# Third attention of a fused four-layer kernel: one reciprocal of few rows for both key blocks, and gathers issued a pair of batches sooner

## The chip, the cores and the metric

The kernel runs on one core of one Trainium2 chip. The metric is the device time of one launch in microseconds; lower is better. Three timed runs of the kernel before are at hand, and one further execution that the hardware profiler took.

## The reference, cut to what matters

The program applies four layers of cross attention and feed-forward to `x` of shape 16 x 128 x 256. The change lies in the attention of the third layer (`L2`), whose input is `x` after the mixture of experts of the second layer has been added to it:

```
q = LN(x @ Wq + bq)                 # 16 heads of 16 channels
k, v         from the first 112 context tokens
k_dca, v_dca from the last  16 context tokens
ctx     = softmax(q k^T / 4)     v          # one softmax over 112 keys
ctx_dca = softmax(q k_dca^T / 4) v_dca      # a second one over 16 keys
x = x + (ctx + ctx_dca) @ Wo + bo
```

So each head of each query has two softmax sums, one for each block of keys, and both outputs have to be divided by their own sum before the output projection adds them. The experts' result reaches `x` by a gather: each token has two rows in a scratch tensor in HBM, and both are added with their weights.

## The kernel before, in words

A stage follows a stage, and in each a Python loop goes over the 16 batches of 128 tokens. Five engines (PE, DVE, ACT, POOL, SP) each work through their own list in order. The framework that builds the kernel chooses each list's order from the program order, from free buffers and from an estimate of its own; so an instruction may stand earlier or later in its list than the code reads.

In the third attention (`l2_attn`) the batch is cut into two halves `c` of eight heads each; within a half, `j` is one of two groups of four heads. For each half:

- `l2_terms` makes the scores `S` of eight heads on PE (in the only buffer of its pool[...]), takes the maxima `mx` of both key blocks and subtracts them on DVE into `E`, and ACT takes the exponent.
- `l2_heads` turns `E` on PE (`pT`), ACT copies it out (`eT`), and PE multiplies it by the values into `po[:, 0]` and by a tile `own` of ones into `po[:, 1]`. The rows of `po` are channels: 32 for each head, 16 of the block of 112 keys and 16 of the block of 16 keys. `own` repeats each sum over its 16 channels, so that the reciprocal `rz` on DVE has a value for every channel (128 x 256), and the product `oT` is one multiplication.
- `l2_out` multiplies `oT` by `Wo` and adds it to `x`.

Around them, `front(b + 3)` makes `qk` and `vx` of a later batch. DVE adds the bias, ACT squares it (`sq`), DVE sums it (`r`) and takes an inverse root in some ten small steps, and POOL scales `qk`. `turn(b + 2)` turns `qk` on PE (`pqkT`), ACT copies it out (`qkT`) and POOL spreads the keys over four heads (`kbd`), from which the next `S` is made. After each even batch `l2_inputs` prepares two more batches. `combine` gathers the experts' rows `moe_y` on the POOL queue (two buffers) and adds them on DVE; then come the statistics `st` and `mv`, the inverse root `rs` on POOL, `xn` on DVE and the turn `pxT` on PE.

Of the kernel before, what the change touches and what calls it, by code (L numbers as in the profile page):

```python
# [8 lines left out]
F32 = mybir.dt.float32  # L9
# [6 lines left out]
ALU = mybir.AluOpType  # L16
# [4 lines left out]
P = 128  # L21
D = 256
# [23 lines left out]
def bc(ap, axis, n):  # L46
    u = ap.unsqueeze(axis)
    shape = list(u.shape)
    shape[axis] = n
    return u.to_broadcast(shape)  # L50


class Net:
# [778 lines left out]
    def l1_ffn(self, w, after, ctx):  # L832
        nc, tc = self.nc, self.tc
# [4 lines left out]
        with ExitStack() as es:  # L838
            op = es.enter_context(tc.tile_pool(name="f1o", bufs=1))
            bp = es.enter_context(tc.tile_pool(name="f1b", bufs=3))  # L840
            sp = es.enter_context(tc.tile_pool(name="f1s", bufs=2))
            tr = es.enter_context(tc.tile_pool(name="f1tr", bufs=3, space=PSUM))
# [145 lines left out]
                pass  # L988
            for _ in late:
                pass  # L990
            self.l2_inputs(0, tr)
            for bs in groups[3:]:
                for _ in shared(bs):
                    pass

    def combine(self, pool, b):

        nc = self.nc
        y = pool.tile([P, 2, D], F32, tag="moe_y", name=f"moe_y{b}")
        for k in range(2):  # L1000
            nc.gpsimd.indirect_dma_start(
                out=y[:, k, :], out_offset=None, in_=self.back,
                in_offset=bass.IndirectOffsetOnAxis(ap=self.slot[:, k, b : b + 1], axis=0),
            )
        for k in range(2):
            nc.vector.scalar_tensor_tensor(
                self.x[b], y[:, k, :], self.pk[:, k, b : b + 1], self.x[b], ALU.mult, ALU.add
            )


    def l2_setup(self, ctx, w):

        nc, tc = self.nc, self.tc
        Wq = w[:, 0:512].rearrange("p (c n) -> p c n", c=2)
        Wm = w[:, 512:1024]
        Wd = w[:, 1024:1536]
        op = ctx.enter_context(tc.tile_pool(name="l2o", bufs=1, side="right"))
        self.l2x = ctx.enter_context(tc.tile_pool(name="l2x", bufs=2, side="right"))

        cd = op.tile([P, B, P], F32, tag="cd", name="cd")  # L1020
        nc.gpsimd.memset(cd, 0.0)
        nc.gpsimd.tensor_copy(cd[:, :, 112:P], self.ctxT[:, :, 112:P])
        nc.gpsimd.memset(self.ctxT[:, :, 112:P], 0.0)

        bqk = op.tile([P, 32, 16], F32, tag="bqk", name="bqk")
        flat = bqk.rearrange("p h d -> p (h d)")

        bv = op.tile([P, 2, 256], F32, tag="bv", name="bv")
        nc.gpsimd.memset(bv, 0.0)
        for t, name, skip, part in (  # L1030
            (flat[:, 256:512], "bkv_main", 0, slice(0, 112)), (flat[:, 256:512], "bkv_dca", 0, slice(112, P)),
            (bv[:, 0], "bkv_main", 256, slice(0, 112)), (bv[:, 1], "bkv_dca", 256, slice(112, P)),
        ):
            at = ROWS[name][0] + skip
            nc.scalar.dma_start(
                out=t[part], in_=self.a["rows"][at : at + 256].partition_broadcast(part.stop - part.start)
            )
        norms = op.tile([P, 6], F32, tag="norms", name="norms")
        nc.scalar.dma_start(out=norms, in_=self.a["norms2"])

        own = op.tile([P, 2, 16], F32, tag="own", name="own")
        nc.gpsimd.tensor_copy(own, self.consts[:, 16:18].unsqueeze(2).to_broadcast([P, 2, 16]))
        nc.vector.tensor_copy(flat[:, 0:256], self.row("bq2"))

        for t in (Wq[:, 0], Wq[:, 1], Wm[:, 0:256], Wd[:, 0:256], flat[:, 0:256], flat[:, 256:512]):
            t3 = t.rearrange("p (h d) -> p h d", h=16)
            m = op.tile([P, 16], F32, tag="wm", name="wm", bufs=2)
            nc.vector.tensor_reduce(m, t3, AX.X, ALU.add)
            nc.vector.tensor_scalar_mul(m, m, 1.0 / 16)
            nc.vector.tensor_tensor(t3, t3, bc(m, 2, 16), ALU.subtract)  # L1050
        self.l2_const = cd, flat, bv, norms, own
        self.l2_xT = {}

    def l2_inputs(self, g, psum):

        bs = [b for b in range(2 * g, 2 * g + 2) if b < self.nb]
        if bs:
            for b in bs:
                self.combine(self.l2x, b)
            xT = self.lnT(self.l2x, psum, bs, rsqrt=self.rsqrt_pool)[1]  # L1060
            for i, b in enumerate(bs):
                self.l2_xT[b] = xT[:, :, i * P : (i + 1) * P]

    def l2_attn(self, w):
        nc, tc = self.nc, self.tc
# [4 lines left out]
        with ExitStack() as es:  # L1070
            sp = es.enter_context(tc.tile_pool(name="l2s", bufs=3))
# [2 lines left out]
            sc = es.enter_context(tc.tile_pool(name="l2sc", bufs=1, space=PSUM))  # L1074
            tr = es.enter_context(tc.tile_pool(name="l2tr", bufs=3, space=PSUM))
            pvp = es.enter_context(tc.tile_pool(name="l2pv", bufs=1, space=PSUM))
            cd, flat, bv, norms, own = self.l2_const
            vp = es.enter_context(tc.tile_pool(name="l2v", bufs=1))
            vx = [vp.tile([P, 16, 2, 16], F32, tag=f"vx{k}", name=f"vx{k}") for k in range(3)]
            xTs, normed, ready = self.l2_xT, {}, {}  # L1080

# [74 lines left out]
            b = self.nb - 1  # L1156
# [28 lines left out]
    def l2_heads(self, sp, ep, tr, pvp, b, c, Es, vx, own, oT):  # L1185

        nc = self.nc
        po = pvp.tile([P, 2, 2, P], F32, tag="po", name=f"po{b}_{c}")
        eTs = []
        for j in range(2):  # L1190
            pT = self.transposes(tr, lambda i: Es[:, j, i, :], 4, f"pT{b}_{c}_{j}")
            eT = ep.tile([P, 4, P], F32, tag="eT", name=f"eT{b}_{c}_{j}", bufs=3)
            nc.scalar.copy(eT, pT)
            eTs.append(eT)
        for j in range(2):
            for of in range(2):
                for i in range(4):
                    stand = own if of else vx[:, 8 * c + 4 * j + i]
                    nc.tensor.matmul(
                        po[32 * i : 32 * i + 32, of, j, :], stand.rearrange("p s d -> p (s d)"), eTs[j][:, i, :],  # L1200
                        start=True, stop=True,
                    )
        rz = sp.tile([P, 2, P], F32, tag="rz", name=f"rz{b}_{c}", bufs=2)
        nc.vector.reciprocal(rz, po[:, 1])  # L1204
        nc.vector.tensor_tensor(oT[:, 2 * c : 2 * c + 2], po[:, 0], rz, ALU.mult)

    def l2_out(self, mm, b, oT, Wo):
        nc = self.nc
# [489 lines left out]
def pack(np, i):  # L1698
# [5 lines left out]
    cat = lambda *x: np.ascontiguousarray(np.concatenate(x, axis=1))  # L1704
    o = {}
# [61 lines left out]
    for name, v in (  # L1767
# [3 lines left out]
    ):  # L1771
        row[ROWS[name][0] : ROWS[name][0] + len(v)] = v
    o["rows"] = row

    o["norms2"] = np.ascontiguousarray(np.stack([
        np.tile(i[f"L2_xattn_{k}"], 8) for k in ("qn_w", "qn_b", "kn_w", "kn_b", "kn_dca_w", "kn_dca_b")
# [9 lines left out]
    c = np.zeros((P, 18), np.float32)  # L1786
# [27 lines left out]
```

## Time and profile before

| | |
|---|---|
| runs, us | 2497.4, 2489.95, 2499.14 (median 2497.4) |
| profiled execution | 2492.25 us, span 2490.5 us, mean granted clock 0.974 |
| busy in the span: PE, DVE, ACT, POOL | 2281.8, 1723.0, 1048.2, 746.9 us |
| from the first to the last reciprocal of the stage | 1395.1 to 1613.7 us |
| reciprocal `rz` of the stage | 32 of 128x256, 1744 ns each |
| multiplication `oT` | 32 of 128x256, 409 ns each |
| gathers `moe_y` | 32, 968 ns each on POOL, 2.8 us to landing |

The page gives busy time of each engine in the span and the costliest groups of instructions by their line. The trace can be cut to a window of time, and asked in it for the busy time of each engine, for what each instruction waited for, and for the instructions in order. A busy PE is not PE at its peak, since matmuls overlap one another. In this trace one product of float32 stands as two rows of PE.

### The profile page before, as it was taken

Reading aid. Unit: us, or ns where it says so; the run is one execution under the profiler, and the core shown is the slowest. Engines: PE = TensorE matmul, PEld = TensorE weight load, DVE = VectorE, ACT = ScalarE, POOL = GpSimd, SP = SyncE. Lnnn points to the kernel's source line nnn. Section 1 sums busy time; section 2 is a strip of 40 time slices with the busy share of each in tenths; the row PEclk is TensorE's granted clock in tenths of the full one; section 3 lists DMA queues with packets and bytes.
Section 4 is the critical chain, followed back from the end, with each engine's and each line's share of the span. In section 5 each row is a group of like instructions: output and inputs, shape, how many; then the busy total and the mean of one; then the engine's idle time right before and its main releaser. Section 6 shows DMA issues by size and latency. Waiting matters only on the chain. (4 is left out here: it accounts for less than half of the span.)

```text
span 2490.5 us, 39604 instructions
## 1 busy us (share of the span) xinstructions
PE 2281.8 (92%) x14876; PEld 1709.7 (69%) x14876; DVE 1723.0 (69%) x3904; ACT 1048.2 (42%) x2778; POOL 746.9 (30%) x678
## 2 busy tenths in 40 slices
PE   6999799999989999998997778899899999999798
PEld 3666589898977777775884455555577777776465
DVE  6888788888865555565574999831466666668964
ACT  3656455455533443432331333411455555554121
POOL 3222234343411322222002433100222332224665
PEclk8999899999999999998999899999999999999999
DMA  9000200000030000002223000000100000000000
GB/s 376 17 2 2 86 1 1 1 1 1 1 121 2 19 10 10 10 13 84 69 71 137 25 14 10 1 0 1 69 1 1 1 1 1 1 1 1 7 13 15
DMA packets 29678, 74.57 MB, mean 30 GB/s; under 512 B 6688, under 2 KB 21160, under 8 KB 23856
## 3 DMA queue, kind: packets, MB, share of 16 engines
q1 hardware_dynamic: 25200, 62.06, 6.7%
q0 software_dynamic: 3072, 8.39, 1.0%
q8 instruction: 119, 1.95, 0.3%
q10 hardware_dynamic: 1216, 1.59, 0.2%
q14 instruction: 71, 0.58, 0.1%
HBM read 46.07 MB, written 25.95 MB: 29 GB/s over the span
## 5 line engine op out<-in xcount | busy, mean ns | idle before, releaser
L501 POOL TENSOR_TENSOR g<-sim 128x1024 f32<-128x1024 f32 x64 | 140.2, 2212 | 221.1 <-ACT sim L466 186.4
L181 PE MATMUL pT<-ident,E 128*128 128x128 f32 x1280 | 196.0, 283 | 9.8 <-POOL E L631 7.5
L511 DVE SCALAR_TENSOR_TENSOR g<-g,th 128x1024 f32<-128x1024 f32 x128 | 194.3, 1577 | 0.0
L181 PEld LDWEIGHTS pT<-ident,E 128*128 128x128 f32 x1280 | 147.0, 144 | 51.7 <-issue 21.8
L507 ACT ACTIVATE g<-sim 128x128 f32<-128x128 f32 x512 | 159.8, 390 | 32.0 <-PE r L525 31.5
L626 ACT ACTIVATE E<-E,mx 128x128 f32<-128x128 f32 x256 | 99.5, 390 | 160.1 <-DVE mx L623 138.7
L1464 POOL TENSOR_TENSOR E<-E,rs 128x512 f32<-128x512 f32 x64 | 66.6, 1041 | 302.0 <-DVE rs L1463 148.6
L1459 ACT ACTIVATE E<-S,mx,sc 128x128 f32<-128x128 f32 x256 | 113.9, 455 | 98.8 <-DVE mx L1455 89.6
L525 PE MATMUL r<-ident,g 128*128 128x128 f32 x1024 | 124.6, 277 | 19.9 <-DVE g L511 19.8
L525 PEld LDWEIGHTS r<-ident,g 128*128 128x128 f32 x1024 | 115.4, 142 | 27.7 <-DVE g L511 17.5
L661 PE MATMUL py<-w_w_l,oT 128*128 128x256 f32 x512 | 128.1, 383 | 5.2 <-DVE x L663 3.6
L1492 PE MATMUL py<-w_w_l,oT 128*128 128x256 f32 x512 | 131.1, 383 | 0.1
L1492 PEld LDWEIGHTS py<-w_w_l,oT 128*128 128x128 f32 x512 | 93.6, 190 | 46.9 <-issue 39.2
L631 POOL TENSOR_TENSOR E<-E,rs 128x512 f32<-128x512 f32 x64 | 66.7, 1042 | 193.5 <-DVE rs L630 119.8
L417 PE MATMUL fh<-xnT,w_w_f 128*128 128x128 f32 x1024 | 122.7, 279 | 0.0
L600 PE MATMUL pt<-xnT,w_w_l 128*128 128x256 f32 x512 | 121.1, 382 | 0.0
L661 PEld LDWEIGHTS py<-w_w_l,oT 128*128 128x128 f32 x512 | 93.9, 190 | 39.4 <-issue 20.1
L417 PEld LDWEIGHTS fh<-xnT,w_w_f 128*128 128x128 f32 x1024 | 118.6, 194 | 1.8
L538 PE MATMUL fy<-w_w_f,wT 128*128 128x256 f32 x512 | 118.4, 379 | 0.0
L1406 PE MATMUL pq<-xnT,w_w_l 128*128 128x256 f32 x512 | 116.2, 380 | 1.0 <-ACT xnT L67 0.6
L600 PEld LDWEIGHTS pt<-xnT,w_w_l 128*128 128x128 f32 x512 | 94.9, 192 | 15.2 <-issue 2.5
L1406 PEld LDWEIGHTS pq<-xnT,w_w_l 128*128 128x128 f32 x512 | 94.8, 190 | 14.4 <-ACT sqk L1372 1.2
(401 smaller groups left out, 5505.7 us busy)
## 6 DMA issues: line engine op xcount, KB each, us to landing
w_w_f<-in_w_f SPq DMA_DIRECT2D x14, 1024.0 KB, 11.2
sent<-zero SPq DMA_DIRECT2D x14, 1024.0 KB, 20.2
w_w_l<-in_w_l SPq DMA_DIRECT2D x14, 1024.0 KB, 11.1
xb<-sent SPq DMA_DIRECT2D x38, 128.0 KB, 2.0
back<-yb SPq DMA_DIRECT2D x38, 128.0 KB, 1.9
x<-in_x SPq DMA_DIRECT2D x16, 128.0 KB, 4.9
out<-x SPq DMA_DIRECT2D x16, 128.0 KB, 1.7
ctx<-in_ctx ACTq DMA_DIRECT2D x1, 1024.0 KB, 8.4
```

Of the source, the lines that this page charges most:

```text
L181: self.nc.tensor.transpose(ps[:, i, :], src(i), self.ident)
L417: nc.tensor.matmul(ps[:, k, :], down[:, c, a * P : (a + 1) * P], xT[:, c, :], start=c == 0, stop=c == 1)
L501: nc.gpsimd.tensor_tensor(g, bc(sim[:, 2 * h, 8 * half : 8 * half + 8], 2, P), bc(sim[:, 2 * h + 1, :], 1, 8), ALU.add)
L507: nc.scalar.activation(g[:, k, :], sim[:, 2 * h + 1, :], AF.Identity, bias=sim[:, 2 * h, a : a + 1])
L511: nc.vector.scalar_tensor_tensor(gf, gf, th[:, h : h + 1], gf, ALU.is_ge, ALU.mult)
L525: nc.tensor.matmul(ps[:, k, :], G[h][:, 4 * q + k, :], self.ident, start=h == 0, stop=h == 3, is_transpose=True)
L538: self.nc.tensor.matmul(py, wT[:, k, :], up[:, a, :], start=a == 0, stop=a == 15)
L600: nc.tensor.matmul(ps[:, k], A[:, h + k, c, :], xT[:, c, :], start=c == 0, stop=c == 1)
L661: nc.tensor.matmul(pys[b], oT[:, j, :], Wo[:, h, :], start=h == 0, stop=h == 15)
L1406: nc.tensor.matmul(ps[:, l], Wq[:, c, h * P : (h + 1) * P], xT[:, c, :], start=c == 0, stop=c == 1)
L1459: nc.scalar.activation(E[:, j, :], S[:, j, :], AF.Exp, bias=mx[:, j : j + 1], scale=sc[:, i, 0, r, j : j + 1], accum_out=rs[:, j : j + 1],)
L1492: nc.tensor.matmul(pys[b], oT[:, j, :], Wo[:, h, :], start=h == 0, stop=h == 15)
```

## The change

Two things change, both inside the third attention.

First, the sums. A tile `sums` that is loaded from HBM takes the place of `own`. Its first part makes PE write the sums of one head into 4 of its 32 rows only (two groups `j` times two key blocks), accumulating both `j` into one tile `po[:, 2]` of 128 x 128. DVE takes the reciprocal of this half-sized tile. Its second part, `spread`, is a matrix of ones and zeros: two more products on PE carry the inverses from those rows to the channels, into a PSUM tile `pr` of the pool that the turns use too. Meanwhile ACT copies the unscaled output from `po[:, 0:2]` to `oT`, and DVE multiplies `pr` by `oT`.

Second, the gathers. `combine` no longer issues its own. `fetch` issues the gathers of a pair of batches when the pair before has been combined, and the first pair's ahead of `l2_inputs(0)`.

```diff
+            self.fetched = {}
+            self.fetch(self.l2x, 0)
             self.l2_inputs(0, tr)
...
+    def fetch(self, pool, g):
+
+        for b in range(2 * g, min(2 * g + 2, self.nb)):
+            y = self.fetched[b] = pool.tile([P, 2, D], F32, tag="moe_y", name=f"moe_y{b}")
+            for k in range(2):
+                self.nc.gpsimd.indirect_dma_start(
+                    out=y[:, k, :], out_offset=None, in_=self.back,
+                    in_offset=bass.IndirectOffsetOnAxis(ap=self.slot[:, k, b : b + 1], axis=0),
+                )
+
+    def combine(self, b):
 
         nc = self.nc
-        y = pool.tile([P, 2, D], F32, tag="moe_y", name=f"moe_y{b}")
-        for k in range(2):
-            nc.gpsimd.indirect_dma_start(
-                out=y[:, k, :], out_offset=None, in_=self.back,
-                in_offset=bass.IndirectOffsetOnAxis(ap=self.slot[:, k, b : b + 1], axis=0),
-            )
+        y = self.fetched.pop(b)
...
-        own = op.tile([P, 2, 16], F32, tag="own", name="own")
-        nc.gpsimd.tensor_copy(own, self.consts[:, 16:18].unsqueeze(2).to_broadcast([P, 2, 16]))
...
             for b in bs:
-                self.combine(self.l2x, b)
+                self.combine(b)
+            self.fetch(self.l2x, g + 1)
             xT = self.lnT(self.l2x, psum, bs, rsqrt=self.rsqrt_pool)[1]
...
+            sums = vp.tile([P, 320], F32, tag="sums", name="sums")
+            nc.scalar.dma_start(out=sums, in_=self.a["sums2"])
+            own = (
+                sums[:, 0:64].rearrange("p (j n) -> p j n", j=2), sums[:, 64:320].rearrange("p (j n) -> p j n", j=2)
+            )
...
-        po = pvp.tile([P, 2, 2, P], F32, tag="po", name=f"po{b}_{c}")
+        own, spread = own
+        po = pvp.tile([P, 4, P], F32, tag="po", name=f"po{b}_{c}")
...
         for j in range(2):
-            for of in range(2):
-                for i in range(4):
-                    stand = own if of else vx[:, 8 * c + 4 * j + i]
-                    nc.tensor.matmul(
-                        po[32 * i : 32 * i + 32, of, j, :], stand.rearrange("p s d -> p (s d)"), eTs[j][:, i, :],
-                        start=True, stop=True,
-                    )
-        rz = sp.tile([P, 2, P], F32, tag="rz", name=f"rz{b}_{c}", bufs=2)
-        nc.vector.reciprocal(rz, po[:, 1])
-        nc.vector.tensor_tensor(oT[:, 2 * c : 2 * c + 2], po[:, 0], rz, ALU.mult)
+            for i in range(4):
+                nc.tensor.matmul(
+                    po[32 * i : 32 * i + 32, j, :], vx[:, 8 * c + 4 * j + i].rearrange("p s d -> p (s d)"),
+                    eTs[j][:, i, :], start=True, stop=True,
+                )
+        for j in range(2):
+            for i in range(4):
+                nc.tensor.matmul(
+                    po[32 * i : 32 * i + 32, 2, :], own[:, j], eTs[j][:, i, :], start=j == 0, stop=j == 1
+                )
+        rz = sp.tile([P, P], F32, tag="rz", name=f"rz{b}_{c}", bufs=2)
+        nc.vector.reciprocal(rz, po[:, 2])
+        nc.scalar.copy(oT[:, 2 * c : 2 * c + 2], po[:, 0:2])
+        pr = tr.tile([P, 2, P], F32, tag="tr", name=f"pr{b}_{c}")
+        for j in range(2):
+            nc.tensor.matmul(pr[:, j], spread[:, j], rz, start=True, stop=True)
+        nc.vector.tensor_tensor(oT[:, 2 * c : 2 * c + 2], pr, oT[:, 2 * c : 2 * c + 2], ALU.mult)
```

The two constant tables that `sums` holds are packed on the host, beside the other weights.

More of the change, by code (lines that the diff above doesn't have):

```diff
@@ L994, in l1_ffn @@
                     pass
-    def combine(self, pool, b):
-        nc = self.nc
-        y = pool.tile([P, 2, D], F32, tag="moe_y", name=f"moe_y{b}")
-        for k in range(2):
-            nc.gpsimd.indirect_dma_start(
-                out=y[:, k, :], out_offset=None, in_=self.back,
-                in_offset=bass.IndirectOffsetOnAxis(ap=self.slot[:, k, b : b + 1], axis=0),
-            )
+    def fetch(self, pool, g):
[7 more added lines that the diff above has]
+    def combine(self, b):
+        nc = self.nc
+        y = self.fetched.pop(b)
         for k in range(2):
@@ L1050, in l2_setup @@
             nc.vector.tensor_tensor(t3, t3, bc(m, 2, 16), ALU.subtract)
-        self.l2_const = cd, flat, bv, norms, own
+        self.l2_const = cd, flat, bv, norms
         self.l2_xT = {}
@@ L1076, in l2_attn @@
             pvp = es.enter_context(tc.tile_pool(name="l2pv", bufs=1, space=PSUM))
-            cd, flat, bv, norms, own = self.l2_const
+            cd, flat, bv, norms = self.l2_const
             vp = es.enter_context(tc.tile_pool(name="l2v", bufs=1))
+            sums = vp.tile([P, 320], F32, tag="sums", name="sums")
[3 more added lines that the diff above has]
+            )
             vx = [vp.tile([P, 16, 2, 16], F32, tag=f"vx{k}", name=f"vx{k}") for k in range(3)]
@@ L1773, in pack @@
     o["rows"] = row
+    own2 = np.zeros((P, 2, 8, 2, 2), np.float32)
+    sp2 = np.zeros((4, 32, 2, 4, 2, 16), np.float32)
+    for j in range(2):
+        own2[:112, j, :, j, 0] = own2[112:, j, :, j, 1] = 1.0
+        for h in range(4):
+            for k in range(2):
+                sp2[h, 2 * j + k, j, h, k, :] = 1.0
+    o["sums2"] = cat(own2.reshape(P, 64), sp2.reshape(P, 2 * P))
     o["norms2"] = np.ascontiguousarray(np.stack([
```

## The prediction, on record before the result

> **What bounds the kernel now.** I read the page first, then the busy time in windows, the waits and the instructions in order, all cut to the third attention, since every edit lies there: the built order of the changed kernel equals the old one on SP, and on the other engines outside this stage, but for one small copy on POOL that goes and one load on the ACT queue that comes. From the first reciprocal of the stage (1395.07 us) to nearly its last, the busy time of each engine was (columns: PE, PE's weight loads, DVE, ACT, POOL):
>
> ```profile
> 1395.07:1610.00 214.93, 177.05 (x1667) 118.50 (x1666) 200.46 (x453) 89.00 (x150) 66.82 (x75) 0.96 0.03 9
> ```
>
> DVE is at 93%, and the reciprocal is its costliest group. The rows of the tile `rz` (min/median/max in ns) give its price at both sizes, since the first attention has the half-sized one:
>
> ```profile
> L361 DVE RECIPROCAL rz<-po x32: 945/948/959, 46.3 to 278.8; 128x128 f32<-128x128 f32 x32
> L1204 DVE RECIPROCAL rz<-po x32: 1739/1744/1758, 1395.1 to 1613.7; 128x256 f32<-128x256 f32 x32
> L1205 DVE TENSOR_TENSOR oT<-po,rz x32: 401/409/425, 1398.1 to 1615.5; 128x256 f32<-128x256 f32 x32
> ```
>
> What DVE waits for in this stretch (total us, times, longest) shows the second half of the change:
>
> ```profile
> DVE xn L154 <- POOL rs L120: 8.9, 4, 3.0
> DVE mx L1177 <- PE S L1168: 4.0, 2, 3.2
> PE pxT L168 <- DVE xn L154: 11.4, 2, 5.7
> PE pxT L168 <- DVE r L1107: 5.4, 2, 2.7
> ```
>
> Four times DVE's list has come to `xn` of a later pair while POOL is still at `kbd`, two gathers and the root. Reciprocals then start 17.75, 13.62, 17.72 and 13.77 us apart, where elsewhere a batch (two reciprocals) takes 12.2 to 13.9 us. One such gap, in the order of instructions:
>
> ```profile
> 1457.44 0.17 DVE L128 TENSOR_SCALAR r_y<-r 128x32 uint32<-128x32 uint32 x1
> ...
> 1457.85 2.03 POOL L1127 TENSOR_TENSOR kbd<-qkT,consts 128x512 f32<-128x512 f32 x2 [2.20 <-issue]
> 1457.93 1.00 DVE L129 TENSOR_SCALAR r_y<-r_y 128x32 uint32<-128x32 uint32 x1
> ...
> 1463.32 0.41 DVE L154 TENSOR_SCALAR xn<-x,mv,rs 128x256 f32<-128x256 f32 x1 [2.94 <-POOL rs L120]
> ...
> 1469.47 1.08 DVE L1177 TENSOR_REDUCE mx<-S 128x8 f32<-128x896 f32 x1
> 1470.47 1.74 DVE L1204 RECIPROCAL rz<-po 128x256 f32<-128x256 f32 x1
> ```
>
> Last, the loop that a batch cannot beat: `pqkT` on PE, `qkT` on ACT, `kbd` on POOL, the next `S`, its maximum. Read the start times in the first column:
>
> ```profile
> 1596.42 0.65 PE L181 MATMUL pqkT<-ident,qk 128*128 128x128 f32 x4 [0.46 <-POOL qk L1109]
> 1597.18 1.26 ACT L1122 ACTIVATE qkT<-pqkT,norms 128x256 f32<-128x256 f32 x3 [3.54 <-PE pqkT L181]
> 1598.57 2.04 POOL L1127 TENSOR_TENSOR kbd<-qkT,consts 128x512 f32<-128x512 f32 x2 [2.20 <-issue]
> 1599.66 1.13 PE L1168 MATMUL S<-kbd,qkT 64*128 64x512 f32 x4 [0.29 <-POOL kbd L1127]
> 1600.84 1.09 DVE L1177 TENSOR_REDUCE mx<-S 128x8 f32<-128x896 f32 x1 [3.24 <-PE S L1168]
> ```
>
> From `pqkT` to `S` are 3.24 us, from `S` to its maximum 1.18.
>
> **The change part by part.** *The reciprocal.* 32 times (1744 - 948) ns are 25.5 us less on DVE. The multiplication keeps its 409 ns: one operand in PSUM, one in SBUF, same size. The products with `own` keep their number.
>
> *What is added.* 32 copies 128x256 from PSUM on ACT, 373 ns each by the row below: 11.9 us on an engine that is at 41%. 64 products 128x128 on PE are 128 rows, 0.12 us each by the row of line 417 (122.7 us for 1024): 15.4 us. The load of `sums` (160 KB) on the ACT queue stands 35 us ahead of its use; nothing waits for it, unless its landing were to take ten times what the page shows for 1024 KB (8.4 us for `ctx`). The copy that made `own` goes from POOL in the experts' stage, where POOL idles.
>
> ```profile
> L417 PE MATMUL fh<-xnT,w_w_f 128*128 128x128 f32 x1024 | 122.7, 279 | 0.0
> L67 ACT COPY xnT<-pxT 128x256 f32<-128x256 f32 x7 | 2.6, 373 | 22.9 <-PE pxT L168 22.9
> ```
>
> *Does PE become the bound?* By busy time it would: 177.05 + 14.9 of the 205 us or less that would be left. The Trainium skill ("Trainium Kernel Development and Optimization", Quick Reference, "Reading a trace") says that matmul busy time misleads, as matmuls are pipelined, and that the share of weight loads is the better one: 118.5 of 214.9, 55%. Counting starts instead of ends in the ordered rows, I get 11.3 us of issue for one changed batch (two times turns 0.88, scores 1.06, values and sums 0.86, spread 0.46; then `qk`, `vx`, `py` and `pqkT` 4.7), below any period here. I take the skill's side: PE bounds nothing by itself, but its order does.
>
> *The new waits.* In the built order PE issues `pr` after the rest of `front`'s products, and behind `pr` stand the turns of the next half (c = 0) or `pqkT`, then the second half of `py` (c = 1). The reciprocal that `pr` waits for stands behind a maximum `mx` of the next scores, which in the old order it preceded. And DVE's list now has `r` straight after `qk`, so that it waits for ACT's exponent and `sq`; before, the long reciprocal and `vx` covered this. ACT's copy of `po` waits for the reciprocal, but nothing behind it is ready sooner. Walking one batch, from one `S` (time 0), durations from the rows above and the ordered rows: maximum from 1.18 to 2.19; sums in `po` ready at 2.13; reciprocal to 3.14; `pr` at 3.35 (three groups of `front`, 1.29 us, are ahead of it); turns at 3.79, copies `eT` 4.54 to 5.61; exponent to 6.67; `sq` to 7.25; `r` to 7.9; maximum to 8.9; reciprocal to 9.85; `pr` at 9.95; `pqkT` at 10.4; next `S` 3.24 later, at 13.64. On DVE the small steps of the inverse root, no longer laid between long ones, end near 15.0, against 14.8 when the next maximum could start. So a plain batch takes 13.7 us where the old one took 12.2 to 13.0: the 1.6 us saved on DVE are lost in this loop.
>
> *The gathers.* The built order has all of them issued by the sixth `kbd` and the roots `rs` two or more `kbd` ahead of their `xn`. I take the 8.9 us of waits as gone, and most of the pair's work on DVE lands in the loop's idle time (behind `qk`, and while `S` is made). In the first five batches about 1.4 us each remain at the end of the list (two combinations of 0.40, statistics 0.34 and 0.09, part of `xn`). Here a rule of the skill speaks against the change ("SBUF — State Buffer", Who interferes with whom): DVE and GpSimd share a port pair as an exclusive lock, and a DVE instruction in a two-port mode, or with two SBUF inputs against one that reads SBUF, blocks until the other ends. The trace agrees: the small step L129 takes 1.00 us as `kbd` runs, L128 of the same shape 0.17; and the 18 combinations of the stage average 708 ns against 479 in the median. All gathers now run on POOL beside combinations. By the rule, if each of 18 were held for a whole `kbd` of 1.04 us, 19 us would be lost; by the trace 18 x 0.23 = 4 us, which the old kernel pays as well. I take the trace, and nothing extra, and keep up to +10 us for the range.
>
> *The sum.* Old: 13 batches from 1395.07 to 1587.20 are 192.1 us. New: five of 13.7 + 1.4 and eight of 13.7 + 0.2 are 186.7: 5.4 less. The batch after it has no `front` and took 14.65 us with a wait of 3.24 us; I give it 12.1: 2.5 less. The last two change by nothing: the halved reciprocal (-0.8) meets the new hop to `pr` and back (+0.75 by `pqkT` to `qkT`). Together -8 us. Against the profiled execution, 2492.25 us, that is 2484; that execution lies 5 us under the median of the runs, 2497.4, so I expect the new median between 2484 and 2489 and say 2487.
>
> A change of 0.5% is 12.5 us, about what a measurement of this kernel can tell from none.
>
> **The rivals.** *DVE stays the bound (0.25).* If the walk is too long at `sq` or `pr` (the scheduler had both ready in its estimate), the time follows DVE's busy time: -25.5 for the reciprocals, -8.9 for the waits, less 5 to 14 us of new idle time on DVE (it idles 14.5 us of the window now): -20 to -30, 2465 to 2475. For it: DVE's 93%; against it: `S` has one buffer, so nothing covers its 1.18 us now.
>
> *Slower (0.13): the loop over `pr`, held up by POOL.* In some batches the built order has the fourth group of `front` ahead of the first `pr` (+0.43), and a small step held by `kbd` as L129 was adds 0.83: 15.0 for a plain batch. If in the five early ones two combinations are held by `kbd` as well (2 x 1.04), they take 18.4. That gives 212 us for thirteen: +20, less 2.5. It decides against the change from 15.0 us for a batch on average, and by more than 12.5 us from 15.9: 2508 to 2513. Against it: L129 now stands ahead of the time of `kbd`.
>
> *The gathers bring nothing (0.17).* The pair's work is 4 us on DVE wherever it stands; if it isn't hidden, only the last batches gain: -3 to +3, 2492 to 2498. For it: the gap of 17.75 us holds only 2.94 us of waiting.
>
> **How the numbers follow.** The likeliest case, a loop of 13.7 us with the waits gone, has 0.45 and a range of its own of 2479 to 2492, mostly within 0.5%. Faster by over 0.5% is the first rival and a fifth of the likeliest: 0.34. Slower by over 0.5%: 0.1. The rest, 0.56, is no change. The range takes in most of the first rival and the milder half of the second: 2466 to 2507.
>
> **What would show it.** Right: `rz` at 948 ns; no `xn <- POOL rs` of more than 1 us after 1400; new waits `r <- ACT sq` of about 1 us a batch, `pr <- DVE rz` on PE of 1 us at c = 1, `mx <- PE S` in most halves; reciprocals of the same half 13.5 to 14 us apart in batches 5 to 12. Wrong: batches of 12.5 us or less with DVE over 90% (first rival), or of over 14.6 us with PE idle ahead of `pr` and POOL late with `kbd` (second).

## The result, and the profile after

The changed kernel takes 2500.04 us (median of 19 runs, 2493.35 to 2502.58), the kernel before 2494.62 us on the same chip (19 runs, 2488.67 to 2499.14). The ratio is 1.0021, with a 95% interval of 1.0014 to 1.0028: 5.4 us slower. The forecast was 2487, some 8 us faster. The time lies in the forecast range and within the 0.5% that was called no change, but it moved the other way. In the profiled executions the span goes from 2490.5 to 2497.2 us. The stage times below are read from one such execution of each kernel.

First the row of the tile `rz` (name, operation, count, min/median/max in ns, first and last start in us). The reciprocal of this stage is now line 1220:

```profile
L1220 DVE RECIPROCAL rz<-po x32: 940/946/958, 1390.7 to 1620.1; 128x128 f32<-128x128 f32 x32
```

Each reciprocal went from 1744 to 946 ns as foreseen, which is 25.5 us of DVE's work. But from the first to the last start are 229.4 us, where there were 218.6. So the stage lost 10.8 us. It began 4.35 us earlier, for a reason that was not traced, and so ended 6.4 us later; the span grew by 6.7.

The same stretch of time as before, by engine (columns: length, then PE, weight loads, DVE, ACT, POOL, and the granted clock):

```profile
1395.07:1610.00 214.93, 186.74 (x1672) 125.34 (x1668) 185.90 (x433) 92.27 (x173) 66.45 (x74) 0.97 0.03 7
```

DVE fell from 200.5 to 185.9 busy us of 214.9. So of the work that the reciprocal gave up, part has become idle time; another part is taken by small steps that now last longer, as a count further down shows. The clock does not explain the loss: it was 0.97 here and 0.96 before. What DVE, PE and ACT wait for in the changed kernel, from 1380 to 1625 us (us in all, times, longest):

```profile
ACT oT L1221 <- DVE rz L1220: 77.2, 26, 4.8
PE pr L1224 <- DVE rz L1220: 17.0, 19, 2.4
DVE r L1118 <- ACT sq L1116: 11.7, 11, 1.9
DVE mx L1189 <- PE S L1180: 7.3, 3, 4.1
```

The row `xn <- POOL rs` is gone (12.6 us, 7 times, before in this window; the 8.9 of the prediction are those from 1395 to 1610), and two rows are new: PE stands before `pr` until the reciprocal is there, and DVE stands before `r` until ACT has squared. One batch in the order of instructions, from a maximum to the next of the same half (the first column is the start; rows between these are left out):

```profile
1560.76 1.28 DVE L1189 TENSOR_REDUCE mx<-S 128x8 f32<-128x896 f32 x2
1561.96 0.94 DVE L1220 RECIPROCAL rz<-po 128x128 f32<-128x128 f32 x1
1562.96 0.71 PE L1224 MATMUL pr<-rz,sums 128*128 128x128 f32 x4 [0.67 <-DVE rz L1220]
1563.51 1.04 PE L181 MATMUL pT<-ident,E 128*128 128x128 f32 x8
...
1566.78 0.69 DVE L1118 TENSOR_REDUCE r<-sq 128x32 f32<-128x512 f32 x1 [1.00 <-ACT sq L1116]
1567.38 1.08 DVE L1189 TENSOR_REDUCE mx<-S 128x8 f32<-128x896 f32 x1
1568.38 0.95 DVE L1220 RECIPROCAL rz<-po 128x128 f32<-128x128 f32 x1
1569.38 0.71 PE L1224 MATMUL pr<-rz,sums 128*128 128x128 f32 x4 [0.41 <-DVE rz L1220]
1569.93 0.60 PE L181 MATMUL pqkT<-ident,qk 128*128 128x128 f32 x4
...
1572.02 2.06 POOL L1139 TENSOR_TENSOR kbd<-qkT,consts 128x512 f32<-128x512 f32 x2 [10.04 <-issue]
1572.20 0.92 DVE L132 TENSOR_TENSOR r_t<-r_t,r_h 128x32 f32<-128x32 f32 x1
...
1573.13 1.13 PE L1180 MATMUL S<-kbd,qkT 64*128 64x512 f32 x4 [0.31 <-POOL kbd L1139]
1573.38 0.74 DVE L133 SCALAR_TENSOR_TENSOR r_y<-r_t,r_y 128x32 f32<-128x32 f32 x1
...
1575.28 0.19 DVE L133 SCALAR_TENSOR_TENSOR r_y<-r_t,r_y 128x32 f32<-128x32 f32 x1
1575.39 1.08 DVE L1189 TENSOR_REDUCE mx<-S 128x8 f32<-128x896 f32 x1
1576.39 0.95 DVE L1220 RECIPROCAL rz<-po 128x128 f32<-128x128 f32 x1
```

In both halves the order on PE is `pr`, then the turns (`pT` after the first `pr`, `pqkT` after the second). From the first `mx` to the next `S` are 12.37 us. The next `mx` comes not 1.18 us after `S` but 2.26, because the root's small steps run last on DVE: two of them last 0.92 and 0.74 us while `kbd` runs on POOL, and the others follow one another alone, 0.22 us apart. The batch takes 14.43 us.

The periods of the stage, as starts of every second reciprocal (worked out from the start times; us):

```
before  12.1 13.2 13.9 13.1 23.1 10.6 19.0 11.3 23.1 10.8 19.2 10.5 12.2 14.6  8.0
after   15.9 15.6 16.4 16.3 16.5 15.1 16.2 14.4 15.4 14.4 15.0 14.4 14.4 15.3  9.6
```

The long batches of before (19 to 23 us, in which a later pair's inputs are made) are gone, and every other batch is longer. The first four lose 11.9 us, the next six win 5.9, the last five lose 4.2.

### The profile page after: what moved, and what is told of

Read it like the earlier page. It is cut to its first block, busy times and chain, and to the rows that moved or that the text cites. A ratio compares the mean times of both kernels' runs of the same rounds, so it can differ in the third digit from the quotient of the medians.

```text
span 2497.2 us, 39904 instructions
## 1 busy us (share of the span) xinstructions
PE 2299.4 (92%) x15004; PEld 1722.6 (69%) x15004; DVE 1714.6 (69%) x3904; ACT 1055.8 (42%) x2810; POOL 747.1 (30%) x677
## 4 chain that ended last, share of the span: by engine, by line
PE 61%; DVE 27%; ACT 5%; POOL 3%; issue 3%; DMA 1%; SPq 0%; POOLq 0%; ACTq 0%; DVEq 0%
DVE g L511 5%; PE r L525 4%; PE pT L181 4%; PE pt L600 4%; PE py L661 4%; PE p L1315 3%; PE po L350 3%; PE py L1512 2%; PE po L645 2%; PE fh L417 2%; PE fy L538 2%; PE py L1323 2%; PE S L617 2%; PE py L1624 2%; PE pu L1611 1%
## 5 line engine op out<-in xcount | busy, mean ns | idle before, releaser
L525 PE MATMUL r<-ident,g 128*128 128x128 f32 x1024 | 124.6, 277 | 19.9 <-DVE g L511 19.8
L1426 PEld LDWEIGHTS pq<-xnT,w_w_l 128*128 128x128 f32 x512 | 94.8, 190 | 14.4 <-ACT sqk L1392 1.2
```

Source lines behind the costliest of these rows:

```text
L525: nc.tensor.matmul(ps[:, k, :], G[h][:, 4 * q + k, :], self.ident, start=h == 0, stop=h == 3, is_transpose=True)
L1426: nc.tensor.matmul(ps[:, l], Wq[:, c, h * P : (h + 1) * P], xT[:, c, :], start=c == 0, stop=c == 1)
```

## The experiments

The names in the expectations: *theory A*, the lists of the engines make a loop over the new hop (reciprocal, `pr`, `pqkT`, `kbd`, `S`) and leave the root's steps alone at its end, and this costs what the reciprocal saves; *rival B*, the added products on PE and copies on ACT cost their own time; *rival C*, the earlier gathers cost time and the sums win; *rival D*, the gathers bring nothing. *Theory A2* came after the first twelve runs: the order follows from the buffer that `pr` takes in the pool `tr`.

All were compared with the kernel before in the same session; the ratio is of this kernel to that one. Where two other kernels are set against each other, the difference is that of their ratios times 2495.

**The two parts of the change, each alone.**

`e1_gathers`: the `po` of four parts, `own` and the product of before; only `fetch`, `combine` and `l2_inputs` are the new ones.

> The earlier gathers alone, with the sums as they were before. Theory A (the new sums' order of DVE's list costs the time, the gathers help): the 8.9 us of waits of xn for rs go, 5 to 12 us faster than before, 2483 to 2490. Rival C (gathers that run beside the combinations on POOL and the shared port cost the time): the wait goes, but the kernel is 3 to 15 us slower than before. Rival D (the gathers bring nothing): within 3 us of before.

Measured: 2493.77 us, ratio 0.9993 (0.9985 to 1.0001): 1.7 us less, or nothing, as rival D has it. DVE's waits in it:

```profile
DVE xn L154 <- POOL rs L120: 8.4, 6, 2.9
```

This is the window from 1380 to 1625 us, in which the kernel before has 12.6. So issuing the gathers sooner takes a third of the waits away and leaves two thirds. The long batches remain too (23.0, 19.2, 23.3, 19.2 us). The gathers bring next to nothing by themselves; the fourth case of the prediction was right on this part.

`e2_sums`: the new `l2_heads` and `sums`, with `combine(pool, b)` of before.

> The new sums alone, with the gathers issued as before. Theory A: the period of a plain batch is 14.4 us as in the changed kernel, and the waits of xn for rs come back in part: 8 to 18 us slower than before. Rival C: 5 us or more faster than before, as the halved reciprocals work without the gathers' cost. Rival D: 3 to 8 us slower, like the changed kernel.

Measured: 2500.66 us, ratio 1.0023 (1.0014 to 1.0033), the time of the whole change. Theory A had the period right and the time too high, rival D the time. The plain batches take 14.4 us, and `xn <- POOL rs` is down to 3.2 us of 12.6. So it is the sums that lose the 5 to 6 us, and also the sums, not the gathers, that took most of the waits away: with them the order of DVE's list is another. In the changed kernel the last combination and statistics of the pairs start by 1453 us, within the first four batches; before, they start as late as 1540.

**How much does the reciprocal bring, and what does the hop cost?**

`e3_nospread` leaves out the products that spread the inverses, the copy on ACT and `pr`. (The table writes the four sums of a head eight times over its 32 rows, so every row holds a sum.) Channels are then multiplied by inverses that are not all their own: the kernel does not compute the attention, and shows only what its time would be without the hop. Slices of `oT` are shortened to `...` here.

```
-        nc.scalar.copy(oT[:, 2 * c : 2 * c + 2], po[:, 0:2])
-        pr = tr.tile([P, 2, P], F32, tag="tr", name=f"pr{b}_{c}")
-        for j in range(2):
-            nc.tensor.matmul(pr[:, j], spread[:, j], rz, start=True, stop=True)
-        nc.vector.tensor_tensor(oT[...], pr, oT[...], ALU.mult)
+        nc.vector.tensor_tensor(oT[...], po[:, 0:2], bc(rz, 1, 2), ALU.mult)
```

> The changed kernel without the spread products, without the copy of po on ACT and without pr: the reciprocals of the few rows are multiplied in as they stand, so the inverses are not spread to the channels. Theory A (the hop from rz over PE to pr, and the order it brings, cost what the shorter reciprocal saves): DVE's list is interleaved as before, a plain batch takes 12 to 12.5 us: 20 to 30 us faster than the changed kernel, 2470 to 2480. If DVE's own steps alone set the time: 5 to 10 us faster, 2490 to 2495.

Measured: 2467.67 us, ratio 0.9886 (0.9871 to 0.9901): 28.4 us faster than before, 34 faster than the changed kernel by the ratios. That is the 25.5 us of the reciprocal, and a little more, when no product stands between it and its use. Reciprocals run from 1394.4 to 1587.1, 192.7 us, and DVE is at 90% again:

```profile
1395.07:1610.00 214.93, 193.66 (x1746) 120.39 (x1745) 194.31 (x509) 94.52 (x158) 72.97 (x86) 0.98 0.03 9
```

**Is it the added work on PE and ACT?**

`e4_moreproducts`:

```
+        for _ in range(2):
+            nc.tensor.matmul(po[:, 3], spread[:, 0], eTs[0][:, 0, :], start=True, stop=True)
         rz = sp.tile([P, P], F32, tag="rz", name=f"rz{b}_{c}", bufs=2)
```

> The changed kernel with two more 128x128 products on PE for each half (64 in all, as many as the change added), written to an unused part of po between the sums and the reciprocal. Rival B (the added products set the time): 64 times 0.12 us, 6 to 9 us slower than the changed kernel, 2506 to 2509. Theory A (order and DVE's steps set it): within 3 us of the changed kernel, 2497 to 2503.

Measured: 2516.29 us, ratio 1.0085 (1.0071 to 1.0098): 16 us slower than the changed kernel, 0.5 us for each half. Both expectations missed it. The expectation priced a product at one row of 0.12 us; the trace shows two rows for each, and two products issue in 0.44 us (from 1539.06 to 1539.49 in one half), which is 14 us for the 64. So they cost about all they take. But the order on DVE and POOL moved with them (`qk` stands ahead of `kbd` in every second batch, which takes 16.0 to 16.1 us), so this run does not separate the products' time from an order. It warns against costing products on PE at nothing here.

**The loop and the list on DVE.**

`e6_rlate`: `r` is queued on DVE behind the second reciprocal.

```
+                with ExitStack() as behind:
+                    if self.rz is not None:
+                        behind.enter_context(tc.issue_after(self.rz.ins))
                     nc.vector.tensor_reduce(r, sq, AX.X, ALU.add)
```

> The changed kernel with the sum of squares r queued on DVE behind the second reciprocal of the batch, so that DVE no longer waits for sq ahead of the maximum. Theory A: the reciprocal of c = 1 comes 5.4 instead of 6.4 us after that of c = 0 and S of the next batch 1 us sooner, but the root's steps then lie beside kbd and end as late as before: between 0 and 8 us faster than the changed kernel, 2492 to 2500. If the wait for sq alone were the cause: 13 us faster, 2487. Rival B: within 3 us of the changed kernel.

Measured: 2495.26 us, ratio 0.9996 (0.9988 to 1.0005), 6 us faster than the changed kernel. The wait for `sq` is gone, plain batches take 14.0, and the root's steps now begin beside `kbd` (one of them took 0.97 us there). As expected, the 1.0 us of the wait comes back in part: 0.4 us of a batch are won.

`e10_root1`: `range(3)` in `rsqrt` becomes `range(1)` for `r`. It leaves out two of the three corrections of the root.

> The changed kernel with one of the three iterations of the inverse root (it leaves out two, six small steps of a batch; the root is then coarse). Theory A: the steps that ran alone at the end of DVE's list are gone, the maximum starts 1.2 us after S, a plain batch takes 13.2 to 13.5 instead of 14.43: 12 to 17 us faster than the changed kernel, 2483 to 2488. If the loop over pr, pqkT and kbd alone set the period: within 3 us of the changed kernel.

Measured: 2493.32 us, ratio 0.999 (0.9981 to 0.9999), 8 us faster than the changed kernel, not 12 to 17. Batches 8 to 14 take 13.2 to 14.1 in place of 14.4 to 15.4: in them the six steps cost the 1.0 us that the rows above show. But the first three batches take 17.9, 20.5 and 18.2 us: DVE's list was ordered anew, with more of the pairs' inputs in them.

`e5_rootpool`:

```
-                r = self.rsqrt(sp, r, 32, "r", b)
+                nc.gpsimd.tensor_tensor(r, r, self.mhalf.to_broadcast([P, 32]), ALU.pow)
```

> The changed kernel with the inverse root of the 32 norms as one power on POOL in place of 12 steps on DVE. Theory A (DVE's list ends late, as the dependent steps of the root stand alone and are held by kbd): the maximum starts 1.2 us after S instead of 2.3, a plain batch takes about 13.3 instead of 14.43, the kernel is 12 to 18 us faster than the changed one, 2482 to 2488. Rival B (the 64 added products on PE and 32 copies on ACT set the period): the period stays at 14.2 to 14.5 and the kernel within 3 us of the changed one, 2497 to 2503.

Measured: 2561.91 us, ratio 1.0273 (1.0259 to 1.0287), 63 us slower than the changed kernel. It tests nothing of the theories, since one power of this size takes 5.4 us, and `kbd` waits behind it:

```profile
L1120 POOL TENSOR_TENSOR r<-r,mhalf x14: 5415/5422/5457, 1391.7 to 1641.0; 128x32 f32<-128x32 f32 x14
```

`e18_poolnewton`: as `e6_rlate`, with the root's iterations as products and additions on POOL.

```
+                eng.tensor_tensor(t, y, y, ALU.mult)
+                eng.tensor_tensor(t, t, h, ALU.mult)
+                eng.tensor_scalar_add(t, t, 1.5)
+                eng.tensor_tensor(y, t, y, ALU.mult)
```

> The kernel with r behind the second reciprocal, with the twelve products and additions of the root's three iterations on POOL (the first guess stays on DVE). Theory A: DVE's list ends with the scores, the maximum starts 1.2 us after S, a plain batch takes 13.0 to 13.4: 2482 to 2488. If POOL's steps are dear (over 0.4 us each, as a power of this size was 5.4 us), kbd comes late behind them and the kernel is slower than the changed one, above 2503.

Measured: 2488.18 us, ratio 0.997 (0.9961 to 0.998), 7.5 us faster than before and 13 faster than the changed kernel. A step costs 0.24 to 0.29 us on POOL. From the fourth batch on a batch takes 12.5 to 13.3, with all added products and copies in it, and in most of their halves the maximum comes 1.18 us after `S`. So the products and copies do not set the 14.43. Against that, the first three batches take 19.1, 18.8 and 19.9 us.

`e22_before_poolnewton`: the same on the kernel before.

> The kernel before with the root's iterations on POOL and nothing else. Theory A (DVE bounds the kernel before, the root's nine steps of 0.19 us are 1.7 us of a batch): 10 to 20 us faster than before, 2476 to 2486, so that the halved reciprocal adds little to it. If the steps fit between others there at no cost: within 3 us of before, 2493 to 2499.

Measured: 2492.05 us, ratio 0.9983 (0.9974 to 0.9992), 4 us faster, between the two expectations. DVE is freed of work, and the waits take it: `rz` waits for `po` 16.4 us in the stage. Freed work on DVE is not time by itself in either kernel.

**Attempts on the order by hand.**

`e12_rlate_turn`: as `e6_rlate`, with `turn(b + 2)` moved ahead of `l2_heads` of the second half.

> The kernel with r behind the second reciprocal, and in addition the turning of the inputs of the batch after next ahead of the second half's sums, so that pqkT, qkT and kbd no longer stand behind pr. Theory A: S of the next batch is made as soon as its bank is free, kbd no longer holds the root's steps: a plain batch takes 12.8 to 13.5 instead of 14.0, 2481 to 2489. If the loop over pr is not what sets the time in that kernel: within 3 us of it, 2492 to 2498.

Measured: 2519.48 us, ratio 1.0093 (1.0077 to 1.0109), 24 us slower than `e6_rlate`. The expectation failed: the two reciprocals of a batch now stand 10.7 to 14.8 us apart in all but the last two batches, where in `e6_rlate` they stood 5.3 to 7.5. `E <- pT` appears as a wait of DVE (22.3 us), and PE waits for `qk` (8.8 us): turns and scores block one another.

`e25_after_gated` and `e21_poolnewton_gated`: `e6_rlate` and `e18_poolnewton`, with a pair's inputs queued behind the second reciprocal.

```
                 if b % 2 == 0:
-                    self.l2_inputs(b // 2 + 2, tr)
+                    with tc.issue_after(self.rz.ins):
+                        self.l2_inputs(b // 2 + 2, tr)
```

> The kernel with r behind the second reciprocal (root on DVE, as in the changed kernel), with the pairs' inputs taken every second batch. Theory A: plain batches stay at 14.0 us, batches with a pair take 15 to 16, so little is won: 0 to 6 us faster than without the gate, 2489 to 2495. If the crowded early batches alone made the change lose: 10 us or more, below 2486.

> The kernel with r behind the second reciprocal and the root's iterations on POOL, and in addition the work on the inputs of each pair queued on DVE behind the second reciprocal of the batch that issues it, so that one pair is taken every second batch and not all of them in the first four. Theory A (in the early batches of that kernel, 19 us each, it is the crowded pairs that cost): the early batches take 13 to 15 us, 8 to 14 us faster than that kernel, 2474 to 2480. If pairs cost the same wherever they stand (4 us of DVE's time each): within 3 us of it, 2485 to 2491.

Measured: 2535.43 us, ratio 1.016 (1.0147 to 1.0174), and 2536.95 us, ratio 1.0166 (1.0152 to 1.018). Both expectations failed by 40 us and more. Batches with a pair take 20 to 27 us. In the first of the two kernels the waits of `xn` for `rs` come to 18.9 us over the stage, and those of `mx` for `S` to 22.7. One of them:

```profile
1401.59 0.41 DVE L154 TENSOR_SCALAR xn<-x,mv,rs 128x256 f32<-128x256 f32 x1 [3.14 <-POOL rs L120]
```

A pair is a chain over DVE, POOL, DVE, PE and ACT. Where its steps follow each other in one batch, DVE stands still between them. As the framework orders them, over the first four batches and among the rest, they are cheaper.

**The buffer of `pr`.** All kernels above that have the hop put `pr` among the tiles of the pool `tr`, from which the turns `pT`, `pqkT` and `pxT` take theirs. `e26_prpo` leaves every product, copy and gather, and lays `pr` in `po`, whose third quarter the reciprocal has read and whose fourth is unused:

```
-        pr = tr.tile([P, 2, P], F32, tag="tr", name=f"pr{b}_{c}")
+        pr = po[:, 2:4]
```

> The changed kernel with pr laid in the second half of po (its sums, which the reciprocal has read, and the unused quarter) in place of a buffer of the pool tr. Products, copies and gathers stay. Theory A2 (pr takes one of three buffers of tr, so the turns of the scores and inputs stand behind it, and the order of DVE's list with them): the root's steps lie between others again, plain batches take 12 to 13 us, 15 to 25 us faster than the changed kernel, 2475 to 2485. Rival B (the products, the copy and the way there and back are the price): within 5 us of the changed kernel, 2495 to 2505.

Measured: 2478.7 us, ratio 0.9933 (0.992 to 0.9947): 16.7 us faster than before and 22 faster than the changed kernel. This version beats both, and it is what theory A2 expected. Its reciprocals run over 203.4 us instead of 229.4. The order of PE in one batch, and what DVE does meanwhile (rows between these are left out):

```profile
1520.10 0.94 DVE L1220 RECIPROCAL rz<-po 128x128 f32<-128x128 f32 x1
...
1520.62 1.13 PE L1180 MATMUL S<-kbd,qkT 64*128 64x512 f32 x4
...
1521.35 0.19 DVE L133 SCALAR_TENSOR_TENSOR r_y<-r_t,r_y 128x32 f32<-128x32 f32 x1
1521.58 0.19 DVE L131 TENSOR_TENSOR r_t<-r_y 128x32 f32<-128x32 f32 x1
1521.68 0.71 PE L1224 MATMUL po<-rz,sums 128*128 128x128 f32 x4
...
1525.27 0.66 PE L181 MATMUL pqkT<-ident,qk 128*128 128x128 f32 x4
1525.63 0.95 DVE L1220 RECIPROCAL rz<-po 128x128 f32<-128x128 f32 x1
1525.86 1.13 PE L1180 MATMUL S<-kbd,qkT 64*128 64x512 f32 x4
1527.11 0.71 PE L1224 MATMUL po<-rz,sums 128*128 128x128 f32 x4
```

Here `pqkT` comes 1.84 us before the `pr` of the same half (now named `po`), `S` comes ahead of `pr` in both halves, and the root's steps run while `S` is made. Over one stretch (columns as above) the changed kernel and then this one:

```profile
1520.00:1580.00 60.00, 54.11 (x493) 36.81 (x494) 51.91 (x119) 27.52 (x52) 12.41 (x12) 1.00 0.01 1
```

```profile
1520.00:1580.00 60.00, 58.65 (x548) 38.79 (x548) 51.96 (x136) 30.32 (x56) 13.79 (x14) 1.00 0.01 1
```

PE does more in the same 60 us (548 matmul records against 493) and is busy for 98% of it; DVE issues 136 instructions instead of 119 in the same busy time. The granted clock was 1.00 in both.

A count says what becomes of the root's steps. Of the 168 rows of `r_h`, `r_y` and `r_t` on DVE that start between 1380 and 1625 us, 12 are longer than 0.3 us in the kernel before, 31 in the changed kernel (26 of them beside `kbd`) and 5 in `e26_prpo`. What these rows last beyond 0.185 us each comes to 6.4, 19.0 and 2.5 us. So the steps meet `kbd` in the order of the changed kernel and hardly in this one. This is of the size of the 22 us, but it is no proof that all of it lies on the path: `e12_rlate_turn` has only 0.4 us of it, and is slow for other waits.

`e30_prpo_oldg`: the same with the gathers of before.

> The same with the gathers issued as before. Theory A2, as the gathers alone were worth 1.4 us before: within 4 us of the kernel with the new gathers, 2475 to 2489. If the early gathers count once DVE is not held elsewhere (9 us of waits for rs): 5 to 10 us slower than with the new gathers.

Measured: 2481.18 us, ratio 0.9953 (0.9939 to 0.9967). By the ratios the new gathers are worth 5.0 us here, by the medians 2.5, and the two intervals overlap: little, though perhaps more than in the old kernel.

`e27_prpo_poolnewton`: `pr` in `po`, the root's iterations on POOL.

> pr in po and the root's three iterations on POOL. Theory A2: DVE is freed of nine steps of a batch, about 1.7 us, and is no longer the bound; the loop over S and its one buffer is: 3 to 10 us faster than with pr in po alone, 2468 to 2480. If POOL is late with kbd behind the root's steps: slower than with pr in po alone.

Measured: 2529.72 us, ratio 1.0139 (1.0123 to 1.0154), 51 us slower than `e26_prpo`: the second expectation's direction. PE now reaches `pqkT` before its input is ready:

```profile
PE pqkT L181 <- POOL qk L1121: 2.8, 4, 1.1
```

```profile
PE pqkT L187 <- POOL qk L1127: 40.6, 13, 8.8
```

The first line is of `e26_prpo`, the second of this kernel. The twelve steps, 4.1 us from the first to `qk` in one batch of `e18_poolnewton` where they run alone, end at `qk`, which PE's list now asks for early. What helped in one order hurts in the other.

`e33_prpo_turn`: `pr` in `po`, `turn(b + 2)` ahead of the second half.

> pr in po, and the turning of the inputs of the batch after next written ahead of the second half's sums. Before, with pr in a buffer of tr, the earlier turn cost 24 us; theory A2 puts that on the buffers of tr, so it costs nothing now: within 5 us of the kernel with pr in po alone. If the earlier turn is bad by itself: 10 us or more slower than that kernel.

Measured: 2491.67 us, ratio 0.9984 (0.9975 to 0.9993), 13 us slower than `e26_prpo`: an early turn is bad by itself, so it was not `pr` among the tiles of `tr` alone that made `e12_rlate_turn` slow.

`e39_prpo_tr2`: `pr` in `po`, and `bufs=2` for the pool `tr` in place of 3.

> pr in po, and tr with two buffers in place of three. If the number of buffers left for the turns is what counts: back to the changed kernel, 2495 to 2505. If it is that turns stand behind a product that waits for the reciprocal: within 8 us of the kernel with pr in po and three buffers, 2475 to 2487.

Measured: 2481.3 us, ratio 0.9931 (0.9917 to 0.9946), that of `e26_prpo`. So it is not the number of buffers left to the turns. That moving `pr` out of `tr` is worth 22 us is shown; why is in part argued. In the changed kernel a turn (`pT` or `pqkT`) follows `pr` on PE in nearly every half, while in `e26_prpo` `pqkT` and `S` pass it in most: the likely reading is that `pr`, which waits for a reciprocal, no longer keeps its place among the turns' tiles. But this order on PE is not enough by itself. `e18_poolnewton` has it too, with `pr` in `tr`, and makes its later batches in 12.5 to 13.3 us; there the root's steps are not at the end of DVE's list. Which of the reorderings carries how much of the 22 us was not separated, and a buffer for `pr` alone, outside both `tr` and `po`, was not tried.

`e34_prpo_root2`: `pr` in `po`, two iterations.

> pr in po, and two iterations of the inverse root instead of three (its last correction is left out). If DVE still bounds the stage: three steps of 0.19 us for 13 batches are 7 us, 2470 to 2475. If PE and the loop over S bound it: within 3 us of the kernel with pr in po alone, 2476 to 2482.

Measured: 2477.81 us, ratio 0.9922 (0.9908 to 0.9935), 2.7 us under `e26_prpo` by the ratios. Three steps fewer on DVE in each batch bring nothing that can be told from zero. It fits the second expectation, that DVE no longer bounds the stage, but does not show it: the two intervals are wide enough for the 7 us of the first.

## Why the prediction went wrong, by its own steps

The account that the runs give, against before: the shorter reciprocal without a hop -28.4; the hop, with `pr` in `po`, +11.7 (0.9933 against 0.9886); `pr` as a tile of `tr`, and the order that this brings, +22. The three add up to the +5.2 of the whole change, but by construction: each is the difference of two ratios in a row, from different sessions, so the sum confirms nothing. What the runs show is the size of each step.

- *The reciprocal* (25.5 us less on DVE): right to 2 ns, and worth its full size in `e3_nospread`.
- *The bound of DVE*: right for the kernel before. The first rival, 2465 to 2475, is where the kernel without the hop came out. The prediction was right to take the hop's loop for the likelier case.
- *The loop over `sq`, `r`, `pr`, `pqkT`, `kbd`*: right. The walk gave 12.46 us from `mx` to the next `S` (13.64 - 1.18); the trace has 12.37, and the points between agree to 0.2 us (first `pr` 2.17 after `mx`, measured 2.20; `pqkT` 9.22, measured 9.17). So this part was right by its mechanism. The new waits are those forecast: `r <- sq` 11.7 us, `pr <- rz` 17.0.
- *The end of DVE's list*: this step failed. The prediction had the root's steps end near 15.0 on the walk's clock, against 14.8 when the maximum could start, thus 0.2 us a batch. It priced them as if laid between others. Measured on the same clock, the last step ends at 15.9 and the maximum starts at 15.8, which is 2.26 us after `S` instead of 1.18 and 1.1 us late. The steps stand 0.22 us apart when alone, and two of them (L132, L133) run into `kbd`. The Trainium skill ("SBUF — State Buffer", Who interferes with whom) says that a DVE instruction with two SBUF inputs contends with a GpSimd instruction that reads SBUF; the trace agrees, as these two took 0.92 and 0.74 us beside `kbd` and 0.19 alone. The prediction knew the rule and named 0.83 us for one step, but kept it for a rival; over the stage such long rows came to 19.0 us, against 6.4 before. The walk also began a period at the `S` that it had found, without carrying the delay into the next round. That these steps are worth about 1 us of a plain batch is shown by `e10_root1`, which leaves six of them out.
- *Plain and early batches*: 13.7 + 0.2 for eight was 111.2 us, measured 119.3. Five early ones of 15.1 were 75.5, measured 80.7. The batch after the thirteenth was to take 12.1, and took 15.3; the last lost 1.6 that had been put at nothing. These are 18.1 us in all; the stage started 4.35 us earlier, which leaves 13.8, against the 13.4 between -8 and +5.4.
- *The gathers* (8.9 us of waits gone): the waits went, but mostly not by the gathers, so this came true for another reason than its own. With the gathers alone 8.4 of 12.6 us stay. The step read `xn <- rs` as a lateness of the gathers; what was late was POOL's `rs`, behind `kbd` (in `e1_gathers` one `kbd` of 2.04 us starts at 1491.57, and `rs` follows it at 1493.57 with no gather between), and DVE had come to `xn` too early. Nor do the other batches of before take 12.2 to 13.9 us throughout, as the prediction read: those right after a long one take 10.5 to 11.3, so part of each gap was made up.
- *PE bounds nothing by itself*: right for the changed kernel, since the batches of 12.5 us with the same products in `e18_poolnewton` show that PE does not set its 14.43. The passage of the Trainium skill ("Trainium Kernel Development and Optimization") on which the prediction leans stands under Performance Expectations there, and it speaks of how close a kernel is to roofline, not of which engine bounds a stage. With the order mended PE is busy for 98% of the stretch, and the hop still costs 11.7 us, most of the 15.4 us of products that the prediction counted as covered. That these 11.7 are PE's was not tried.
- *The slower rival* had the right place (steps held by `kbd`; the fourth group of `front` ahead of the first `pr`, which is so in the first six batches) and an early batch that was too dear: 18.4 against 15.6 to 16.5. Its break-even of 15.0 us a batch agrees: the mean of the first thirteen was 15.4.

Something was missing altogether: the prediction noted that turns stand behind `pr`, and took this as given by the product. It did not ask why the order was so. `pr` was given a tile of the turns' pool, one line, and with this line changed the same kernel is 22 us faster, four times what the change lost.

## What to carry to other kernels

When a result makes a hop over another engine, ask which pool its tile comes from: here a tile that waits for a slow operation was 22 us dearer in the pool from which the quick ones take theirs than in a free part of a tile that was already its own. When a freed engine has small dependent steps, price them alone and beside the operations that lengthen them (here `kbd`), since the long operations that covered them are what the change takes away. Every edit reorders the lists of all engines here, so read a change's worth from a run that leaves out only the suspected part, not from the busy time that it frees.

## What was not expected of the hardware

- A power on POOL grows with its columns: 128x32 takes 5.42 us (`e5_rootpool`), where the 128x2 one of `rs` takes 0.72. A product of 128x32 takes 0.24 (`e18_poolnewton`).
- Two products 128x128 with f32 operands are four rows in the trace and take 0.44 us of PE's issue, 0.22 each (`e4_moreproducts`, and `pr` of the changed kernel).
- Dependent steps of 128x32 on DVE start 0.22 us apart, though a row alone says 0.17 to 0.19; laid between other work they cost about 0.1 (in `e26_prpo` one starts at 1549.68 and the next instruction at 1549.78). While `kbd` runs on POOL, one takes up to 0.98 us (L131 of the changed kernel).
